# When the last expert's tokens are finished: a mixture-of-experts layer with all outputs written before the last expert is added, and the chosen rows written again by a scatter

## The chip, the cores and the metric

The kernel runs on one core of a Trainium2 chip. The core has five engines that run side by side, each with its own queue of instructions: TensorE (PE: matrix products), VectorE (DVE), ScalarE (ACT), GpSimd (POOL) and SyncE (SP, which here only issues transfers). The metric is the device time of one execution in microseconds (us); lower is better. Line numbers such as L1570 are lines of the kernel before.

## What is computed

4 sequences of 1024 tokens of 256 numbers, float32 (4096 tokens in all), pass two attention layers and two feed-forward layers. Each of the four is applied as `x = x + layernorm(layer(layernorm(x)))`. Only the last is touched by the change. It is a mixture of eight experts in which the experts choose tokens:

```
xt = layernorm(x).reshape(4096, 256)
S  = sigmoid(xt @ Wg).T                # 8 experts x 4096 tokens
G, I = top_k(S, 1024)                  # each expert takes 1024 tokens
hid = gelu(xt[I] @ W1[e] + b1[e])      # 256 -> 1024
out = (hid @ W2[e] + b2[e]) * G        # 1024 -> 256
new = zeros.at[I].add(out)             # a token may have several experts, or none
x = x + layernorm(new)
```

## The kernel before

The tokens stand in SBUF for the whole run, as eight blocks `xs[0]` to `xs[7]` of 512 tokens (128 partitions x 4 x 256). Normalised rows and the gate scores go to a table in device memory, `tok_d`; a second table, `acc_d`, of 4096 rows of 256, starts at zero and collects the experts' sums.

The experts run one after the other, each in two halves of 512 tokens (`feed_forward(u)`, u from 0 to 15; expert e = u // 2). For an expert, GpSimd gathers its 1024 rows from `tok_d` in eight chunks of 128 (`got`, L1493). A half then does this: TensorE turns four chunks to `xT` (L1516, copied by VectorE, L1518), computes `ph` for eight slices of the hidden layer (L1534, 16 matmuls in two per slice, three PSUM buffers), ScalarE applies Gelu (L1541), and TensorE computes `py` for each of the four chunks (L1556, two PSUM buffers). VectorE adds the bias (L1568) and multiplies by the gate (L1569), and GpSimd adds the chunk's rows to `acc_d` with an accumulating scatter (L1570). The turning of the next half's chunks stands on TensorE between the second and third, and the third and fourth, `py`.

The orders on PE, DVE and ACT are written out by hand: within this part an engine runs its instructions in the order in which the code issues them. GpSimd's and SP's queues are laid out by a scheduler. Scatter-adds of different chunks into `acc_d` wait for one another, except those of the last expert, whose tokens are distinct.

After the experts stands a separate last part (L1598 to L1647). Every read of `acc_d` waits for all scatters of the last expert (`last_scatters`); then, block by block:

- SP reads the block's sums back to SBUF (`back`, L1610)
- VectorE computes mean and variance of each token (`bn_stats`, `bn_aggr`, in `ln_stats`, L179 to L182), GpSimd raises the variance to the power -1/2 (L184) and multiplies it by the negative mean (L1631)
- ScalarE applies the scale and shift (L1619), and the result is added to `xs[t]` and stored: for the first four blocks by an accumulating transfer into the output (L1645), to which the rows of `xs[t]` were stored during the attention layer (L1166, `ADDED = 4`); for the others by an add on GpSimd or VectorE (L1624) and a store (L1625).

Of the kernel before, what the change touches and what calls it, by code (L numbers as in the profile page):

```python
# [9 lines left out]
F32 = mybir.dt.float32  # L10
I32 = mybir.dt.int32
BF16 = mybir.dt.bfloat16
AF = mybir.ActivationFunctionType
# [5 lines left out]
P = 128  # L19
D = 256  # L20
# [25 lines left out]
CAP = 2  # L46
NSEG = P // NE
NROUND = 15
ADDED = 4


def bucket_runs():
# [19 lines left out]
def kernel(  # L72
# [956 lines left out]


    tok_d = dram.tile([NT, D + NE], F32, name="tok_d")
    spare = const.tile([P, 1], F32, name="spare")
    with ExitStack() as st3:

# [83 lines left out]
        def close(t, h, oT):  # L1118
# [43 lines left out]
                return scale_of("g", xs[t][:, i, :])  # L1162

            def token_rows(i, mean, rs):
                if t < ADDED:
                    nc.sync.dma_start(out_flat[t][:, i, :], xs[t][:, i, :])  # L1166
                if i == 0:
                    gating["h"] = wk.tile([P, NJ, D], F32, tag="hg", name="hg")
                hg = gating["h"][:, i, :]
                nc.vector.tensor_scalar(hg, xs[t][:, i, :], mean, rs, ALU.subtract, ALU.mult)  # L1170
                nc.sync.dma_start(tok_d[t * TB + i * P : t * TB + (i + 1) * P, 0:D], hg)
                if i % 2:
                    beside.append(lambda: turn_gating(i - 1))
                if i == NJ - 1:
                    beside.append(gate)
# [133 lines left out]
    with ExitStack() as st4:  # L1309
# [132 lines left out]
        class List:  # L1442
# [43 lines left out]
            def gather(self):  # L1486
                nc.tensor.matmul(parts[:, P : P + NC], lhsT=self.listed, rhs=fold, start=True, stop=True)  # L1487
                self.idx = wk.tile([P, NC], I32, tag="idx", name="idx")
                nc.vector.tensor_copy(self.idx, parts[:, P : P + NC])  # L1489
                self.got = []  # L1490
                for c in range(NC):
                    g = wk.tile([P, D + NE], F32, tag="got", name="got", bufs=2 * NC)
                    nc.gpsimd.indirect_dma_start(  # L1493
                        out=g,
                        out_offset=None,
                        in_=tok_d[:, :],
                        in_offset=bass.IndirectOffsetOnAxis(ap=self.idx[:, c : c + 1], axis=0),
                        bounds_check=NT - 1,
                        oob_is_err=True,
                    )  # L1500
                    self.got.append(g)

        lists = [List(e) for e in range(NE)]
        last_scatters = []
        QPE = NC // NJ
        xT = {}

# [12 lines left out]
        def feed_forward(u):  # L1520
# [6 lines left out]
            for h in range(TB // n):  # L1527
# [3 lines left out]
                for f in range(FC):  # L1531
# [12 lines left out]
                    if coming is not None and h == TB // n - 1:  # L1544
                        if f == 1:
                            coming.chunks()
                        elif 2 <= f < 6:
                            coming.places(f - 2)
            if coming is not None:
                for part in range(4):  # L1550
                    coming.collect(part)
            for i in range(NJ):
# [11 lines left out]
                    coming.gather()  # L1564
                if i in (1, 2) and u + 1 < NE * QPE:
                    turn(u + 1, i - 1)
                y = wk.tile([P, D], F32, tag="y", name="y", bufs=4)
                nc.vector.tensor_tensor(y, py, mb2[:, e, :], ALU.add)  # L1568
                nc.vector.tensor_scalar(y, y, lists[e].got[k][:, D + e : D + e + 1], None, ALU.mult)  # L1569
                scatter = nc.gpsimd.indirect_dma_start(  # L1570
                    out=acc_d[:, :],
                    out_offset=bass.IndirectOffsetOnAxis(ap=lists[e].idx[:, k : k + 1], axis=0),
                    in_=y,
                    in_offset=None,
                    bounds_check=NT - 1,
                    oob_is_err=True,
                    compute_op=ALU.add,
                )
                if e == NE - 1:

                    for other in last_scatters:
                        tc.declare_no_dep(scatter.ins, other.ins, reason="an expert's tokens are distinct")
                    last_scatters.append(scatter)

        lists[0].chunks()
        for part in range(4):
# [1 line left out]
            lists[0].collect(part)  # L1588
        lists[0].gather()
        for u in range(NE * QPE):  # L1590
            feed_forward(u)
            e, q = divmod(u, QPE)
            if q == QPE - 1 and e + 2 < NE:
                weights.append(load_expert(e + 2))

    out_rows = out.flatten_outer_dims().rearrange("(t p j) d -> t p j d", p=P, j=NJ)  # L1598
    with ExitStack() as st5:
        wk = st5.enter_context(tc.tile_pool(name="back", bufs=1))  # L1600
        st5.enter_context(tc.manual_schedule(engines={engines.DVE, engines.Activation}))
        all_rows = mybir.DependencyInfo(mybir.DependencyClass.Sync, mybir.DependencyReason.DATA)
        ys = []
        for t in range(NB):
            y = wk.tile([P, NJ, D], F32, name=f"back{t}")
            rows = "(p j) d -> p j d" if t < ADDED else "(j p) d -> p j d"
            acc_t = acc_d[t * TB : (t + 1) * TB, :].rearrange(rows, p=P)

            for js in (slice(0, 1), slice(1, NJ)) if t == 0 else (slice(0, NJ),):
                read = nc.sync.dma_start(y[:, js, :], acc_t[:, js, :])  # L1610
                for scatter in last_scatters:
                    tc.add_manual_dep(read.ins, scatter.ins.name, all_rows, reason="all rows")
            ys.append(y)

        HALVES = (slice(0, NJ // 2), slice(NJ // 2, NJ))

        def apply_on_act(t, tiles, rs, ms):
            for i in tiles:
                nc.scalar.activation(  # L1619
                    ys[t][:, i, :], ys[t][:, i, :], AF.Identity, bias=ms[:, i : i + 1], scale=rs[:, i : i + 1]  # L1620
                )

        def add(t, eng, js):
            eng.tensor_tensor(xs[t][:, js, :], xs[t][:, js, :], ys[t][:, js, :], ALU.add)  # L1624
            nc.sync.dma_start(out_flat[t][:, js, :], xs[t][:, js, :])  # L1625

        for t, y in enumerate(ys):
            mv, rs = ln_stats("c", [y[:, i, :] for i in range(NJ)])
            ms = small.tile([P, NJ], F32, tag="msc", name="msc")
            nc.vector.tensor_scalar(ms, mv[:, :, 0], -1.0, None, ALU.mult)  # L1630
            nc.gpsimd.tensor_tensor(ms, ms, rs, ALU.mult)  # L1631
            if t == NB - 1:

                add(t - 1, nc.vector, slice(0, NJ))
                for i in range(NJ // 2):
                    nc.vector.tensor_scalar(
                        y[:, i, :], y[:, i, :], mv[:, i, 0:1], rs[:, i : i + 1], ALU.subtract, ALU.mult
                    )
                apply_on_act(t, range(NJ // 2, NJ), rs, ms)
                for js in HALVES:  # L1640
                    add(t, nc.vector, js)
                continue
            apply_on_act(t, range(NJ), rs, ms)
            if t < ADDED:
                nc.gpsimd.dma_start(out_rows[t], y, accum_op=ALU.add)  # L1645
            elif t < NB - 2:
                add(t, nc.gpsimd, slice(0, NJ))  # L1647


# [32 lines left out]
```

## The time and the profile before

Three runs had a median of 1663.57 us (1662.66 to 1664.27). The profiled execution took 1663.55 us; its span, from the first to the last instruction that the profile shows, was 1661.6 us at a mean granted TensorE clock of 0.966.

| engine | busy, us | share of the span | instructions |
|---|---|---|---|
| PE (matmul) | 1544.9 | 93% | 8663 |
| DVE | 913.8 | 55% | 2050 |
| ACT | 634.0 | 38% | 1099 |
| POOL | 390.5 | 23% | 419 |

| the end of the span | us from its start |
|---|---|
| expert 7, first half: first `ph` | 1566.4 |
| expert 6's last scatter issued | 1571.1 |
| expert 7, second half: first `ph` | 1594.8 |
| last `py` ends | 1622.6 |
| last scatter issued | 1623.7 |
| first statistics of the last part | 1630.1 |
| last add ends | 1658.3 |
| span ends | 1661.6 |

How to read rows of the timeline: start in us, duration in us, engine, line, operation, what it writes and reads, how many; in brackets how long the engine was idle before, and what ended that. A page's group rows give busy time and the mean duration in ns.

### The profile page before, as it was taken

The page shows a single profiled execution, that of the slowest core. Times are in us where ns is not written, and L with a number is a line of the kernel's source. Part 1 is how long each engine was busy: PE and PEld are TensorE (multiplying, and loading weights), DVE is VectorE, ACT ScalarE, POOL GpSimd, SP SyncE. Part 2 cuts the span into 40 slices and gives each one's busy share as a digit, 9 for nine tenths or more (in the row PEclk, how much of TensorE's full clock was granted, in tenths as well). Part 3 has the DMA queues.
Part 4 walks back from the last instruction along what each step waited for, and adds up shares of the span by engine and source line. Part 5 has one row for each costly group of instructions (what it writes and reads, how often), then busy time and mean ns, then how long its engine had stood idle before and what let it go on. Part 6 is the DMA issues. An engine that isn't in the chain of part 4 may idle for free.

```text
span 1661.6 us, 22279 instructions
## 1 busy us (share of the span) xinstructions
PE 1544.9 (93%) x8663; PEld 769.6 (46%) x8663; DVE 913.8 (55%) x2050; ACT 634.0 (38%) x1099; POOL 390.5 (23%) x419
## 2 busy tenths in 40 slices
PE   7999999999999999999999999914999999999990
PEld 4666666675223232323232222203766766667670
DVE  4555556664567777778787878775121222212115
ACT  3344444544554545454545464421112121121213
POOL 4222233222102011111010101012332432433325
PEclk9999999999999999999999999956999999999995
DMA  8300000000000000000000000030233323423217
GB/s 210 109 1 1 1 1 1 1 1 0 1 1 1 17 11 17 11 14 14 14 14 1 14 8 7 28 128 26 65 68 73 69 66 74 95 47 79 32 19 209
DMA packets 66196, 64.31 MB, mean 39 GB/s; under 512 B 23181, under 2 KB 60074, under 8 KB 65962
## 3 DMA queue, kind: packets, MB, share of 16 engines
q1 hardware_dynamic: 52352, 42.81, 8.4%
q0 software_dynamic: 12864, 19.14, 6.9%
q8 instruction: 68, 1.11, 0.3%
q10 hardware_dynamic: 874, 0.93, 0.2%
q14 instruction: 38, 0.31, 0.1%
HBM read 39.64 MB, written 23.23 MB: 38 GB/s over the span
## 4 chain that ended last, share of the span: by engine, by line
PE 90%; issue 3%; DVE 3%; POOL 2%; DMA 1%; ACT 1%; SPq 0%; POOLq 0%; ACTq 0%; DVEq 0%
PE sc L1223 16%; PE po L1239 15%; PE py L1556 13%; PE ph L1534 13%; PE py L792 3%; PE pg L684 3%; PE pv L700 3%; PE pt L1127 2%; PE ph L848 2%; PE po L764 2%; PE pv L373 2%; PE pq L349 2%; PE pq L869 2%; PE po L768 2%; PE pk L349 1%
## 5 line engine op out<-in xcount | busy, mean ns | idle before, releaser
L1233 DVE TENSOR_SCALAR w<-sc 128x1024 f32<-128x1024 f32 x256 | 312.8, 1222 | 97.3 <-PE sc L1223 65.1
L1232 ACT ACTIVATE w<-sc 128x512 f32<-128x512 f32 x512 | 277.9, 595 | 229.7 <-PE sc L1223 102.6
L1223 PE MATMUL sc<-qT,kT 32*128 32x512 f32 x2048 | 293.6, 640 | 1.5 <-ACT w L1232 0.8
L1239 PE MATMUL po<-w,vaug 128*17 128x512 f32 x2048 | 274.7, 598 | 1.3 <-DVE turned L1271 0.3
L1556 PE MATMUL py<-w,hid 128*128 128x256 f32 x1024 | 230.1, 380 | 0.0
L1541 ACT ACTIVATE hid<-ph,mb 128x512 f32<-128x512 f32 (+1 forms) x136 | 90.0, 662 | 365.7 <-PE ph L1534 365.7
L1534 PE MATMUL ph<-xT,w 128*128 128x512 f32 (+1 forms) x544 | 225.0, 572 | 0.5 <-DVE xT L1518 0.4
L1556 PEld LDWEIGHTS py<-w,hid 128*128 128x128 f32 x1024 | 191.2, 190 | 31.9 <-issue 7.5
L1223 PEld LDWEIGHTS sc<-qT,kT 32*128 32x128 f32 x2048 | 80.8, 183 | 184.9 <-issue 170.7
L1534 PEld LDWEIGHTS ph<-xT,w 128*128 128x128 f32 x544 | 104.8, 193 | 111.6 <-issue 107.6
L1570 POOL DMA_INDIRECT acc_d<-y,idx x64 | 100.8, 1575 | 212.3 <-issue 151.2
L1568 DVE TENSOR_TENSOR y<-py,mb 128x256 f32<-128x256 f32 x64 | 26.8, 419 | 184.4 <-PE py L1556 184.4
L1239 PEld LDWEIGHTS po<-w,vaug 128*17 128x17 f32 x2048 | 35.3, 95 | 200.3 <-issue 171.0
L1493 POOL DMA_INDIRECT got<-tok_d,idx x64 | 65.8, 1028 | 152.7 <-DVE idx L1489 135.6
L1518 DVE COPY xT<-tp 128x512 f32<-128x512 f32 (+1 forms) x34 | 22.4, 660 | 96.8 <-PE tp L1516 96.8
L1059 POOL TENSOR_TENSOR rsg<-veg,mhalf 128x1 f32<-128x1 f32 x32 | 17.7, 553 | 219.5 <-DVE veg L1058 219.5
L792 PE MATMUL py<-wo,oT 128*128 128x256 f32 x256 | 61.9, 385 | 0.0
L684 PE MATMUL pg<-nT,wh 128*128 128x512 f32 x128 | 60.5, 604 | 1.5 <-ACT nT L623 1.5
L700 PE MATMUL pv<-wh,nT 128*128 128x512 f32 x128 | 59.7, 593 | 0.0
L1489 DVE CAST idx<-parts 128x8 int32<-128x8 f32 x8 | 1.3, 167 | 101.8 <-PE parts L1487 101.8
L792 PEld LDWEIGHTS py<-wo,oT 128*128 128x128 f32 x256 | 47.4, 190 | 17.2 <-issue 9.4
L565 POOL TENSOR_TENSOR x<-x,y 128x1024 f32<-128x1024 f32 x14 | 32.9, 2352 | 73.3 <-ACT y L554 73.3
(262 smaller groups left out, 1854.0 us busy)
## 6 DMA issues: line engine op xcount, KB each, us to landing
w<-in_L_ffn_W_dram SPq DMA_DIRECT2D x16, 1024.0 KB, 5.7
x<-in_L_attn_x_dram SPq DMA_DIRECT2D x8, 512.0 KB, 5.0
acc_d<-logits SPq DMA_DIRECT2D x8, 512.0 KB, 5.0
tok_d<-hg SPq DMA_DIRECT2D x32, 128.0 KB, 1.8
back<-acc_d SPq DMA_DIRECT2D x7, 512.0 KB, 8.9
out_dram<-x SPq DMA_DIRECT2D x16, 128.0 KB, 1.7
out_dram<-back POOLq DMA_DIRECT2D x4, 512.0 KB, 6.5
out_dram<-x SPq DMA_DIRECT2D x3, 512.0 KB, 3.2
```

What stands on the lines that cost most here:

```text
L684: nc.tensor.matmul(pg, lhsT=wh[:, c, HID + e * P : HID + (e + 1) * P], rhs=d["nT"][:, c, :], start=(c == 0), stop=(c == DC - 1),)
L700: nc.tensor.matmul(pv, lhsT=d["nT"][:, c, i * P : (i + 1) * P], rhs=wh[:, c, 0:HID], start=(c == 0), stop=(c == DC - 1),)
L792: nc.tensor.matmul(py, lhsT=d["oT"][:, e, :], rhs=wo[:, e, :], start=(e == 0), stop=(e == EC - 1))
L1223: nc.tensor.matmul(sc, lhsT=row["kT"][t][rows, r, kt * P : (kt + 1) * P], rhs=row["qT"][rows, t, qh * TB : (qh + 1) * TB], start=True, sto ...
L1232: nc.scalar.activation(w[:, j, :], sc, AF.Relu)
L1233: nc.vector.tensor_scalar(w[:, 2:4, :], pair, 0.0, None, ALU.max)
L1239: nc.tensor.matmul(po[32 * j : 32 * j + HD + 1, :], lhsT=row["v"][:, kt, HQ * t + 2 * j + r, :], rhs=w[:, j, :], start=(kt == 0), stop=(kt ...
L1493: nc.gpsimd.indirect_dma_start(out=g, out_offset=None, in_=tok_d[:, :], in_offset=bass.IndirectOffsetOnAxis(ap=self.idx[:, c : c + 1], axi ...
L1534: nc.tensor.matmul(ph, lhsT=w1[:, c, f * P : (f + 1) * P], rhs=xT[u][:, c, h * n : (h + 1) * n], start=(c == 0), stop=(c == DC - 1),)
L1541: nc.scalar.activation(hid[:, f, h * n : (h + 1) * n], ph, AF.Gelu, bias=mb1[:, e * FC + f : e * FC + f + 1])
L1556: nc.tensor.matmul(py, lhsT=hid[:, f, i * P : (i + 1) * P], rhs=w2[:, f, :], start=(f == 0), stop=(f == FC - 1),)
L1570: scatter = nc.gpsimd.indirect_dma_start(out=acc_d[:, :], out_offset=bass.IndirectOffsetOnAxis(ap=lists[e].idx[:, k : k + 1], axis=0), in_ ...
```

## The change

The sums in `acc_d` without the last expert are complete once expert 6's last scatter has landed. The change finishes all tokens from these sums while the last expert runs, and finishes the 1024 tokens that the last expert chose a second time, in SBUF, with its contribution:

- While attention runs, the blocks `xs[t]` are stored to a new table `x_d`; the early stores to the output are gone, and so is `ADDED`.
- In expert 6, after its first half, GpSimd gathers the rows of `x_d` that expert 7 chose (`xg`, eight chunks).
- At the start of expert 7 SP reads six blocks of `acc_d` into free buffers (two more later), and GpSimd gathers the chosen rows of `acc_d` (`accg`, eight chunks).
- Between the steps of expert 7, at places set by a table (`asides`), the eight blocks get statistics, power, scale, add and store; the chosen chunks get the bias times the gate (`chosen_known`).
- In expert 7 `py` times the gate is added to `accg` in one VectorE operation, in place of bias, gate and scatter-add. The chunks of its first half are finished during the second half, those of the second half one by one (`chosen_out`): statistics, power, subtraction, multiplication and addition to `xg`, and a plain scatter of the rows over the output. The first of these scatters waits for all block stores.
- The separate last part is gone.

TensorE's instructions and their order are the same as before. The order of the steps in the last expert, by the code: block statistics 0 and 1 follow Gelu 6 and 7 of the first half; statistics 2 to 5 follow its four `py`, and 6 and 7 follow Gelu 0 and 1 of the second half. ScalarE's two halves of a block's scaling come one and two places later, the second of them with the block's add and store.

```diff
             def token_rows(i, mean, rs):
-                if t < ADDED:
-                    nc.sync.dma_start(out_flat[t][:, i, :], xs[t][:, i, :])
...
+                if i == NJ - 1:
+                    nc.sync.dma_start(x_d[t * TB : (t + 1) * TB, :].rearrange("(j p) d -> p j d", p=P), xs[t])
...
+        def stats_of(tag, tiles):
...
+            for i, s in enumerate(tiles):
+                nc.vector.bn_stats(st[:, i, :], s)
+            for i in range(n):
+                nc.vector.bn_aggr(mv[:, i, :], st[:, i, :])
+            nc.vector.tensor_scalar(ve[:, :n], mv[:, :n, 1], EPS, None, ALU.add)
+            nc.gpsimd.tensor_tensor(rs[:, :n], ve[:, :n], mhalf[:, :n], ALU.pow)
+            return mv, rs
+
+        def read_back(t):
+            y = room_back[t % len(room_back)]
+            nc.sync.dma_start(y, acc_d[t * TB : (t + 1) * TB, :].rearrange("(j p) d -> p j d", p=P))
+            ys[t] = [y]
+
+        def all_stats(t):
+            y = ys[t][0]
+            mv, rs = stats_of("c", [y[:, i, :] for i in range(NJ)])
+            ms = few.tile([P, NJ], F32, tag="msc", name="msc")
+            nc.vector.tensor_scalar(ms, mv[:, :, 0], -1.0, None, ALU.mult)
+            nc.gpsimd.tensor_tensor(ms, ms, rs, ALU.mult)
+            ys[t] += [rs, ms]
+
+        def all_scaled(t, half):
+            y, rs, ms = ys[t]
+            for i in (2 * half, 2 * half + 1):
+                nc.scalar.activation(
+                    y[:, i, :], y[:, i, :], AF.Identity, bias=ms[:, i : i + 1], scale=rs[:, i : i + 1]
+                )
+
+        def all_out(t):
+            nc.vector.tensor_tensor(xs[t], xs[t], ys[t][0], ALU.add)
+            stores.append(nc.sync.dma_start(out_flat[t], xs[t]))
+            if t + len(room_back) < NB:
+                read_back(t + len(room_back))
+
+        def chosen_known(ks):
+            for k in ks:
+                nc.vector.scalar_tensor_tensor(
+                    accg[:, k, :], mb2[:, NE - 1, :],
...
+        def chosen_out(ks):
+            mv, rs = stats_of("d", [accg[:, k, :] for k in ks])
+            for i, k in enumerate(ks):
+                nc.vector.tensor_scalar(accg[:, k, :], accg[:, k, :], mv[:, i, 0:1], None, ALU.subtract)
+            for i, k in enumerate(ks):
+                nc.vector.scalar_tensor_tensor(
+                    xg[:, k, :], accg[:, k, :], rs[:, i : i + 1], xg[:, k, :], ALU.mult, ALU.add
+                )
+                scatter = nc.gpsimd.indirect_dma_start(
+                    out=out_rows,
+                    out_offset=lists[NE - 1].at_chunk(k),
+                    in_=xg[:, k, :],
...
+                for store in stores:
+                    tc.add_manual_dep(scatter.ins, store.ins.name, over, reason="in the place of")
...
+        def with_last_rows():
+            for c in range(NC):
+                lists[NE - 1].fetch(xg[:, c, :], x_d, c)
+
+        def with_last_acc():
+            for tag in ("w1", "w2"):
+                free = we.tile([P, 2, NJ, D], F32, tag=tag, name=f"back_{tag}")
+                room_back.extend(free[:, k] for k in range(2))
+            room_back.extend(wk.tile([P, NJ, D], F32, tag="back", name="back") for _ in range(2))
+            for t in range(len(room_back)):
+                read_back(t)
+            for c in range(NC):
+                lists[NE - 1].fetch(accg[:, c, :], acc_d, c)
+
+        def asides():
...
+            places = [(0, "f", 6), (0, "f", 7), *((0, "i", i) for i in range(NJ)), (1, "f", 0), (1, "f", 1)]
+            later = [(0, "f", 7), *((0, "i", i) for i in range(NJ)), (1, "f", 0), (1, "f", 1), (1, "f", 2)]
+            latest = [*((0, "i", i) for i in range(NJ)), (1, "f", 0), (1, "f", 1), (1, "f", 2), (1, "f", 3)]
+            for t in range(NB):
+                put(later[t], lambda t=t: all_scaled(t, 0))
+                put(latest[t], lambda t=t: all_scaled(t, 1), lambda t=t: all_out(t))
+                put(places[t], lambda t=t: all_stats(t))
+            put((0, "f", 7), lambda: chosen_known((0, 1)))
+            put((0, "i", 0), lambda: chosen_known((2, 3)))
+            put((1, "f", 4), lambda: chosen_known((4, 5)))
+            put((1, "f", 5), lambda: chosen_known((6, 7)), lambda: chosen_out((0, 1, 2, 3)))
...
-                y = wk.tile([P, D], F32, tag="y", name="y", bufs=4)
-                nc.vector.tensor_tensor(y, py, mb2[:, e, :], ALU.add)
-                nc.vector.tensor_scalar(y, y, lists[e].got[k][:, D + e : D + e + 1], None, ALU.mult)
...
+                gates = lists[e].got[k][:, D + e : D + e + 1]
+                if e < NE - 1:
...
+                else:
+                    nc.vector.scalar_tensor_tensor(accg[:, k, :], py, gates, accg[:, k, :], ALU.mult, ALU.add)
+                    aside(u, "i", i)
+                    if q:
+                        chosen_out((k,))
...
         for u in range(NE * QPE):
+            if u == (NE - 1) * QPE:
+                with_last_acc()
             feed_forward(u)
             e, q = divmod(u, QPE)
+            if u == (NE - 1) * QPE - 2:
+                with_last_rows()
...
-    with ExitStack() as st5:
```

The last line stands for the whole last part, L1598 to L1647, which is removed.

## The prediction, made before the changed kernel ran

> **What bounds the kernel now.** I read the page first: TensorE is busy 93% of the span, and the chain that ended last is 90% PE. The change cannot shorten TensorE's work, so I looked for where TensorE is not the chain. In the timeline's last 100 us that is the stretch after its last matmul:
>
> ```profile
> 1608.58 13.98 PE L1556 MATMUL py<-w,hid 128*128 128x256 f32 x64
> 1623.68 1.55 POOL L1570 DMA_INDIRECT acc_d<-y,idx  x1 [1.90 <-DVE y L1569]
> 1627.86 6.79 SPq L1610 DMA_DIRECT2D back<-acc_d  x9
> 1631.62 0.43 DVE L179 BATCH_NORM_STATS2 stc<-back 128x6 f32<-128x256 f32 x1 [0.87 <-DMA back<-acc_d]
> 1656.97 1.32 DVE L1624 TENSOR_TENSOR x<-x,back 128x512 f32<-128x512 f32 x2
> ```
>
> TensorE ends at 1622.56; the span ends at 1661.6. These 39.0 us are the prize: the last scatter must land (1627.5), all of acc_d is read back, and eight blocks are normalised and added. The waits on SP's queue say what holds it, in total, times and longest us: the last expert's scatters.
>
> ```profile
> SPq L1610 <- DMA acc_d<-y,idx: 119.6, 3, 112.6
> ```
>
> What the change must fit into is the last expert: its first half begins at 1566.42, its second at 1594.84, and nothing of it waits today. The second thing to see is GpSimd's queue before that, in expert 6:
>
> ```profile
> 1557.50 1.55 POOL L1570 DMA_INDIRECT acc_d<-y,idx  x1 [2.97 <-issue]
> 1562.11 1.55 POOL L1570 DMA_INDIRECT acc_d<-y,idx  x1 [3.05 <-issue]
> 1566.72 1.55 POOL L1570 DMA_INDIRECT acc_d<-y,idx  x1 [3.06 <-issue]
> 1571.14 1.55 POOL L1570 DMA_INDIRECT acc_d<-y,idx  x1 [2.87 <-issue]
> ```
>
> Each scatter-add waits for the one before to land, one per 4.5 us. The queue is behind (the y for the last was ready at 1567.4), so any work put between them moves the last one.
>
> **Removed.** Of the 39.0 us tail, what must remain after the last matmul is one chunk: accg (0.46), its statistics (0.85: 0.43, 0.18, 0.17 and gaps), the power (0.55, the mean of L1059's 128x1), xg (0.46), 0.3 to issue, the landing (2.8 for a gather, 3.8 for a scatter-add; I take 3.5) and 1.0 to the end of the program (the last store's landing to 1661.6): 7.1 us. Were all else hidden, the span would be about 1630, a gain of 32. The rest of this part is why I do not expect that.
>
> **Added before the last expert.** (1) x_d: eight 512 KB stores replace sixteen of 128 KB on SP's queue, during attention, where DMA moves 1 GB/s in most slices; the last runs beside the weight loads near 1090, but its rows are first needed long after the gathers at 1143.6. Cost 0; if exposed, one landing of 5. (2) Eight gathers of xg. In the built order they stand in GpSimd's queue four after expert 6's first scatter-add and four after its second. One gather takes 1.01 plus 0.30, so four take 5.2, more than the 2.9 that the queue waits anyway; a scatter-add behind gathers is also followed later (5.94 from 1538.00 to 1543.94, against 4.5). Second at 1545.2, third at 1552.3, then 5.9 and four times 4.5: the last at 1576.2 instead of 1571.14. Plus 5.1.
>
> **Added in the last expert.** Now I walk the four queues in built order.
> - GpSimd: eight gathers of accg wait for that scatter-add (1576.2 + 4.5 = 1580.7), and take 8 x 1.31: until 1591.2. The power of block 0 stands behind them. That is the first trouble: power (1.05 alone, mean 1.27 in L184; I take 1.4), product 0.3, so ms of block 0 is there at 1592.9.
> - DVE: block 0 is read by about 1584 (3.7 from issue before), statistics of a block 2.2 (2.4 in the old interleaved order), two of them and two known chunks (0.42 each, STT rows of L1147 less overlap), then accg of py 0 at 1589.4 to 1589.9. TensorE's third py needs that PSUM buffer and started at 1587.39 before: 2.6 late.
> - ACT scales block 0 (4 x 0.52) until 1595.0, and only then DVE can add it: the add (1.23, L1624 of 128x1024) stands in DVE's queue ahead of statistics 2, two known chunks, the xT copy (0.69) and accg of py 1. So the copy ends at 1600.1 and accg of py 1 at 1600.5; TensorE's fourth py waits for it until 1600.6, and behind one more add (1.23) and statistics (2.2) the second xT copy ends at 1604.7. TensorE starts the second half at 1604.3 instead of 1594.84: 9.5 late.
> - Second half: 18 scaling operations are ahead of the first Gelu on ACT, and two stand ahead of and two behind each of the next three, each waiting on DVE's statistics and the power. ph has three PSUM buffers. DVE is now the pace: add + statistics = 3.4, 3.5 to 4 a block with waits. Adds end: block 0 1596.3, block 3 1610.3, block 7 1626.3. Gelu 3 is done at 1624.0, so the last ph ends at 1627.5 instead of 1608.6: 19 us late.
> - Then on DVE: four known chunks 1.7, statistics of four chunks 2.1, four subtractions 1.3, first xg 1631.9; scatters from 1632.1. The store of block 7 has landed by then (1626.3 + 3.2 to 4.5). The plain scatter has no row: I bound it by the gather (1.01 + 0.30) and the scatter-add (1.55 + 0.30), and take the gather's, which does not accumulate either. The four end at 1637.4; the power of chunk 4 is queued behind them; then each chunk goes round power 0.55, xg 0.5, issue 0.28, scatter 1.31 = 2.65. TensorE's last py, done near 1642.5, is not late for that. Scatters of chunks 4 to 7 issue at 1638.8, 1641.4, 1644.1 and 1646.7; plus 3.5 and 1.0.
>
> Sum: span 1651.2, against 1661.6: 10.4 less. From 39.0 - 7.1 = 32 hoped for, 19 go to the late second half and 2 to 3 to chunks queued on GpSimd. Profiled time before is 1663.55, 1.95 over its span, and the median 1663.57: so 1651.2 + 1.95 = 1653.2.
>
> **Two rules weighed against rows.** The shared port. Two pairs of rows from two places:
>
> ```profile
> 1654.06 1.23 DVE L1624 TENSOR_TENSOR x<-x,back 128x1024 f32<-128x1024 f32 x1 [3.30 <-ACT back L1619]
> 1654.17 1.99 POOL L184 TENSOR_TENSOR rsc<-vec,mhalf 128x4 f32<-128x4 f32 x1
> ...
> 1080.26 0.67 POOL L1059 TENSOR_TENSOR rsb<-veb,mhalf 128x1 f32<-128x1 f32 x1 [0.19 <-DVE veb L1058]
> 1080.36 0.48 DVE L1147 SCALAR_TENSOR_TENSOR y<-y,mvb,gam 128x256 f32<-128x256 f32 x1
> ```
>
> The power behind an add waited for it (1.99); the add behind a power did not wait (0.48, its usual time), and the power grew by 0.12. The Trainium skill, SBUF — State Buffer, "SBUF: two separate sides", says that a vector operation with two SBUF inputs and a GpSimd operation that reads SBUF exclude each other for a whole instruction, whoever starts first. By the rule every block's add would also stand behind power and product: 1.25 a block over seven intervals, +9, span 1660; by the row 0 to 0.4. I take the row (hence the 1.4).
>
> The clock. Windows of 2 us around one short pause of TensorE (us, busy of PE, PEld, DVE, ACT, POOL, granted clock, DMA):
>
> ```profile
> 1070.00:1072.00 2.00, 0.55 (x2) 0.53 (x3) 1.36 (x2) 0.00 (x0) 0.00 (x0) 0.95 0.00 0
> 1072.00:1074.00 2.00, 2.00 (x6) 1.55 (x6) 0.00 (x0) 0.00 (x0) 0.00 (x0) 0.50 0.00 0
> 1074.00:1076.00 2.00, 2.00 (x8) 1.65 (x7) 1.34 (x3) 0.00 (x0) 0.00 (x0) 0.70 0.01 3
> 1076.00:1078.00 2.00, 1.88 (x13) 0.92 (x13) 1.47 (x5) 0.58 (x1) 0.03 (x1) 1.00 0.37 129
> ```
>
> A pause of 2.3 us halved the clock and some 3.5 us of work restored it. TensorE: Matmul & The Clock Gate, "Part 1", says an idle window of about 3.4 us throttles; the row says that less can. Here the pauses are 7 us (before the fourth py) and 2.5 us (between ph's). The ph's at 3.4 still fit ACT's pace of 4; the last two and the first py run half: about +2, mostly hidden behind the four scatters. By the rule 0, by the row 0 to 2.
>
> **Rivals.**
> 1. Slower: the clock stays halved to the end. If pauses recur so that four py take 27.6 rather than 13.8, the last py ends at 1627.5 + 3.4 + 27.6 = 1658.5 and the chunk's 7.1 follow: 1665.6, 1667.6 us. It turns to a loss when the second half's py run at half clock for more than 10 of their 14 us. Against it: those four are gapless once the Gelus are there, and the rows recover within 4.
> 2. The port excludes, as the page has it: span 1660, 1662 us, nothing gained; with powers of 1.99 for each, 1666.7.
> 3. Better: expert 6's queue absorbs the gathers (-5), and statistics pack to 2.0: 1644 span, 1646 us.
> 4. The end hides as hoped, because ACT and DVE never make TensorE wait: 1632 us. Against it: DVE's added work alone (eight statistics, eight adds, eight chunks) is some 46 us and cannot begin before 1584.
>
> **Chances.** My schedule within 4 us 0.52; better 0.24; hoped-for end 0.03; port 0.13; slower clock or several costs at their upper ends 0.08. Measurement tells about 0.2% (3.3 us) from no change. Faster by more than that (below 1660.2) 0.86, same 0.08, slower 0.06. The range holds all but the hoped-for end, the slower clock and the last of the port case: 1642 to 1661.5.
>
> **To look for after.** TensorE: a wait before the fourth py of the last expert's first half, released by DVE accg, and ph's about 4 us apart in the second, released by ACT hid. GpSimd: eight accg gathers from about 1581, the first power after them; last scatter-add near 1576. Scatters at the end 2.6 apart. Wrong: if TensorE runs through (then the time is near 1632), if adds are 5.5 apart (port), if py rows are 0.8 us each at a clock of 0.5 to the end.

## The result and the profile after

The changed kernel takes 1651.2 us (median of four runs, 1650.42 to 1651.57); the kernel before took 1663.4 beside it. The ratio is 0.9925, with a 95% interval of 0.9913 to 0.9938: 12 us faster. The forecast was 1653.2, in a range from 1642 to 1661.5. The span of the profiled execution is 1648.8 us, 12.8 less than before, at a granted clock of 0.974.

The last 100 us of the timeline, as before the change (start, duration, engine, line, operation):

```profile
1565.45 13.90 PE L1669 MATMUL ph<-xT,w 128*128 128x512 f32 x32
...
1588.44 3.72 PE L1692 MATMUL py<-w,hid 128*128 128x256 f32 x16 [1.76 <-DVE accg L1718]
...
1597.79 6.29 PE L1692 MATMUL py<-w,hid 128*128 128x256 f32 x16 [5.19 <-DVE accg L1718]
1603.92 7.27 PE L1669 MATMUL ph<-xT,w 128*128 128x512 f32 x16
1611.74 1.98 PE L1669 MATMUL ph<-xT,w 128*128 128x512 f32 x4 [0.56 <-ACT hid L1676]
1617.35 8.46 PE L1669 MATMUL ph<-xT,w 128*128 128x512 f32 x12 [3.63 <-ACT hid L1676]
1625.65 13.98 PE L1692 MATMUL py<-w,hid 128*128 128x256 f32 x64
...
1642.55 1.05 POOL L1579 DMA_INDIRECT out_dram<-xg,idx  x1 [0.81 <-DVE xg L1576]
```

Two sums are to be read here. After TensorE's last matmul (1639.63) only 9.2 us are left, where there were 39.0: 29.8 gained. But that last matmul was at 1622.56 and is now 17.1 later: 29.8 - 17.1 = 12.7, which is, but for rounding, the difference of the spans. TensorE, which had never waited in the last expert, now waits 1.76 + 5.19 + 0.56 + 3.63 = 11.1 us, and behind the long waits it is slow: 6.29 us for a product that takes 3.72.

GpSimd's queue answers to the four scatter-adds shown of before:

```profile
1551.55 1.63 POOL L1708 DMA_INDIRECT acc_d<-y,idx  x1 [0.30 <-issue]
...
1574.44 1.56 POOL L1708 DMA_INDIRECT acc_d<-y,idx  x1 [2.94 <-issue]
1579.03 1.08 POOL L1499 DMA_INDIRECT accg<-acc_d,idx  x1 [3.03 <-DMA acc_d<-y,idx]
...
1588.36 1.01 POOL L1499 DMA_INDIRECT accg<-acc_d,idx  x1 [0.30 <-issue]
1589.39 1.06 POOL L1530 TENSOR_TENSOR rsc<-vec,mhalf 128x4 f32<-128x4 f32 x1
```

The last scatter-add is 3.3 us later than before (1571.14), although this run reached expert 7 one microsecond sooner (1565.45 against 1566.42). The power of block 0 starts as the last gather of accg ends. SP's wait for the scatter-adds (in total, times, longest) is now one, not three. Behind it the block stores (L1555) wait for VectorE, which makes their rows:

```profile
SPq L1535 <- DMA acc_d<-y,idx: 71.4, 1, 71.4
SPq L1555 <- DVE stc L1526: 31.0, 6, 12.2
```

The chain of waits, in order of time (start, duration, what), says what then set the end:

```profile
1588.36 1.01 POOL accg L1499
1589.39 1.06 POOL rsc L1530
...
1592.87 1.23 DVE x L1554
1594.10 1.31 DVE stc L1526 x4
...
1605.17 2.02 POOL rsc L1530
...
1609.15 0.99 ACT back L1549 x2
1610.17 1.23 DVE x L1554
...
1616.73 0.58 ACT hid L1676
1617.35 8.46 PE ph L1669 x12
1625.82 13.83 PE py L1692 x64
```

From the gathers it goes through VectorE, GpSimd and ScalarE round after round, one round for each block, and only then through TensorE, for the last ph's and the last products. VectorE's and GpSimd's steps for the last chunk follow (left out here). The experiments take this chain apart.

### The profile page after: what moved, and what is told of

The parts are those of the page before. It is cut to its first block, busy times and chain, and to the rows that moved or that the text cites. A ratio compares the mean times of both kernels' runs of the same rounds, so it can differ in the third digit from the quotient of the medians.

```text
span 1648.8 us, 22341 instructions
## 1 busy us (share of the span) xinstructions
PE 1550.9 (94%) x8663; PEld 770.9 (47%) x8663; DVE 926.6 (56%) x2090; ACT 634.3 (38%) x1101; POOL 399.7 (24%) x434
## 5 line engine op out<-in xcount | busy, mean ns | idle before, releaser
L1669 PE MATMUL ph<-xT,w 128*128 128x512 f32 (+1 forms) x544 | 228.5, 578 | 4.7 <-ACT hid L1676 4.2
L1708 POOL DMA_INDIRECT acc_d<-y,idx x56 | 88.5, 1580 | 166.5 <-issue 139.5
L1706 DVE TENSOR_TENSOR y<-py,mb 128x256 f32<-128x256 f32 x56 | 23.4, 418 | 142.8 <-PE py L1692 135.5
L791 PE MATMUL py<-wo,oT 128*128 128x256 f32 x256 | 61.9, 385 | 0.0
```

Source lines behind the costliest of these rows:

```text
L791: nc.tensor.matmul(py, lhsT=d["oT"][:, e, :], rhs=wo[:, e, :], start=(e == 0), stop=(e == EC - 1))
L1669: nc.tensor.matmul(ph, lhsT=w1[:, c, f * P : (f + 1) * P], rhs=xT[u][:, c, h * n : (h + 1) * n], start=(c == 0), stop=(c == DC - 1),)
L1708: nc.gpsimd.indirect_dma_start(out=acc_d[:, :], out_offset=lists[e].at_chunk(k), in_=y, in_offset=None, bounds_check=NT - 1, oob_is_err=Tr ...
```

## The experiments

All are the changed kernel with the edit shown, timed in three rounds beside the kernel before, whose median lay between 1663.75 and 1664.14. Ratios are to it. `behind(a, b)` only puts a after b in GpSimd's queue. Starts of expert 7 differ by up to 1.7 us between the profiled runs, before any edit reaches TensorE; so the last column counts from there. The intervals reach some 2 to 3 us to each side: differences of 1 to 2 us between two rows rest on that column and on the ranges of the four runs of each.

| kernel | time, us | ratio, 95% interval | last scatter, us after expert 7's first `ph` |
|---|---|---|---|
| changed kernel | 1651.2 | 0.9925 [0.9913, 0.9938] | 77.1 |
| block finishing left out | 1633.3 | 0.9817 [0.9801, 0.9834] | 59.1 |
| xg gathers spread | 1644.9 | 0.9888 [0.9872, 0.9905] | 70.2 |
| powers first | 1646.4 | 0.9895 [0.9879, 0.9912] | 72.2 |
| products first | 1654.2 | 0.9939 [0.9922, 0.9955] | 79.9 |
| statistics first | 1647.7 | 0.9903 [0.9887, 0.992] | 73.4 |
| TensorE kept busy | 1650.3 | 0.9921 [0.9905, 0.9938] | 75.7 |
| three orders together | 1639.1 | 0.9851 [0.9835, 0.9868] | 65.3 |
| and Gelus ahead | 1636.4 | 0.9834 [0.9818, 0.9851] | 62.4 |
| and chosen chunks early | 1636.7 | 0.9838 [0.9822, 0.9855] | 62.5 |
| Gelus ahead, end pipelined | 1635.0 | 0.9827 [0.9811, 0.9844] | 61.0 |

**1. What the block finishing costs.** The eight blocks' read back, statistics, scaling, add and store are left out; the chosen rows are finished as in the changed kernel.

```
-            for t in range(NB):
-                put(later[t], lambda t=t: all_scaled(t, 0))
-                put(latest[t], lambda t=t: all_scaled(t, 1), lambda t=t: all_out(t))
-                put(places[t], lambda t=t: all_stats(t))
...
-            for t in range(len(room_back)):
-                read_back(t)
```

> The finishing of the eight blocks is left out of the last expert: no reads of the sums by blocks, no statistics, scaling, add or store (rows that the last expert did not choose are not written); gathers, chosen chunks and scatters stay. Theory (the block steps on VectorE and ScalarE, standing ahead of what TensorE waits for, make the second half 18 us late): TensorE runs almost through, its last py ends near 1624, and the 9.2 us that follow it in the changed kernel's profile give 1635 us. Rival (the gathers on GpSimd and the chunks queued behind scatters are what costs): 1645 us or more.

The timeline of TensorE and the last scatter:

```profile
1595.15 13.90 PE L1663 MATMUL ph<-xT,w 128*128 128x512 f32 x32
1608.88 13.98 PE L1686 MATMUL py<-w,hid 128*128 128x256 f32 x64
1625.77 1.04 POOL L1579 DMA_INDIRECT out_dram<-xg,idx  x1 [0.82 <-DVE xg L1576]
```

No wait is left in TensorE's rows. The finishing that was meant to run beside the last expert costs 17.9 us there, and the scheme without it would gain 30. So the change is a gain of 30 less a bill of 18. The remaining runs ask what the bill is for: work, or order.

**2. GpSimd's queue ahead of the last expert.** The eight gathers of xg, four and four behind two scatter-adds of expert 6, stand one behind each.

```
                         compute_op=ALU.add,
                     )
+                    if e == NE - 2:
+                        if k:
+                            behind(scatter, fetched[-1])
+                        fetched.append(lists[NE - 1].fetch(xg[:, k, :], x_d, k))
+                        behind(fetched[-1], scatter)
...
-            if u == (NE - 1) * QPE - 2:
-                with_last_rows()
```

> The eight gathers of xg stand one behind each scatter-add of expert 6, in the pauses of about 3 us in which GpSimd waits for a landing, instead of four and four behind the first two. Theory (expert 6's last scatter-add, 4.3 late because of them, moves everything behind it): the last scatter-add is back near 1570, all adds come 4 us earlier, 1647 us. Rival (VectorE's and ScalarE's order paces the last expert whatever the start): 1650 to 1652 us.

GpSimd's timeline: a gather now fits into the time for which the queue waits for a landing anyway.

```profile
1565.30 1.59 POOL L1713 DMA_INDIRECT acc_d<-y,idx  x1 [1.70 <-DMA acc_d<-y,idx]
1567.20 1.06 POOL L1499 DMA_INDIRECT xg<-x_d,idx  x1 [0.31 <-issue]
1569.83 1.59 POOL L1713 DMA_INDIRECT acc_d<-y,idx  x1 [1.56 <-DMA acc_d<-y,idx]
1571.73 1.06 POOL L1499 DMA_INDIRECT xg<-x_d,idx  x1 [0.31 <-issue]
1573.82 1.02 POOL L1499 DMA_INDIRECT accg<-acc_d,idx  x1 [1.03 <-DMA acc_d<-y,idx]
```

The last scatter-add is 4.6 us sooner, the first gather of accg 5.2, and the kernel 6.3, 2 more than the theory had. Counted from expert 7's start, the first add comes 5.8 us sooner and the last one 5.5; the rest of the gain is at the end, where the last chunks wait for TensorE no more (0.3 and 0.9 us in the changed kernel). Eight gathers are the same work; their place was worth all they cost.

**3. GpSimd's queue in front of the first power.** Powers and products of blocks 0 and 1 stand ahead of the last four gathers of accg, which are needed much later.

```
-            for c in range(NC):
-                lists[NE - 1].fetch(accg[:, c, :], acc_d, c)
+            fetch_acc(range(4))
...
+            put((0, "f", 7), lambda: fetch_acc(range(4, NC)), lambda: chosen_known((0, 1)))
```

> On GpSimd the powers and products of blocks 0 and 1 stand behind four of the eight gathers of accg instead of behind all eight. Theory (the first add waits for gathers that nothing needs yet): first power near 1584.5 instead of 1589.4, first add near 1588.4 instead of 1592.9, 1647 us. Rival (a later wait takes its place, the scalings ahead of the Gelus): no more than 1 us, 1650 us.

As the theory had it: 4.8 us less. The first power starts at 1586.51, in a run that reached expert 7 1.7 us later than the changed kernel did, and the second half starts at 1599.67 instead of 1603.92.

**4. TensorE's second half started sooner, and nothing else.** VectorE's block steps of the first half's four products stand behind the fourth product instead of between them.

```
+            known = at[0, "i", 0].pop()
+            at[0, "i", NJ - 1] = [step for i in range(NJ) for step in at.pop((0, "i", i))]
+            at[0, "i", 0] = [known]
```

> On VectorE the block steps of the first half (adds and statistics between the py) all stand behind the fourth product of py with the gate, so that the copies of xT and the products come first; ScalarE's order is unchanged. Theory (VectorE's sum of work and the 18 scalings ahead of the first Gelu pace the second half, not its start): TensorE starts the second half near 1595 instead of 1603.9 but then waits for the first Gelu; the time stays within 2 us of 1651. Rival (TensorE's late start sets the end): 8 us less, 1643 us.

The timeline shows what became of the 5.8 us (counted from expert 7's start) by which the second half is earlier:

```profile
1599.72 5.31 PE L1672 MATMUL ph<-xT,w 128*128 128x512 f32 x12
1615.00 5.59 PE L1672 MATMUL ph<-xT,w 128*128 128x512 f32 x8 [9.96 <-ACT hid L1679]
```

TensorE fills its three PSUM buffers and then waits 9.96 us for the first Gelu, which stands on ScalarE behind the scalings of blocks 0 to 3 and two of block 4. The kernel is 3 us slower by the medians (its four runs, 1651.8 to 1655.1, all lie above the changed kernel's), 1 more than the theory allowed, and the rival's gain of 8 is out. TensorE's late start in the changed kernel is therefore a symptom: the chain of the blocks sets the pace. A block step put off is lost in part: from expert 7's start the first add is 5.8 us later, the last one 4.2, the last scatter 2.8.

**5. The loop in that chain.** A block's statistics stand ahead of the scalings and the add of the blocks before it, at each place of the last expert.

```
             for t in range(NB):
+                put(places[t], lambda t=t: all_stats(t))
+            for t in range(NB):
                 put(later[t], lambda t=t: all_scaled(t, 0))
                 put(latest[t], lambda t=t: all_scaled(t, 1), lambda t=t: all_out(t))
-                put(places[t], lambda t=t: all_stats(t))
```

> One ordering is changed: at each place of the last expert the next block's statistics stand ahead of the block before's scalings and add, not behind them. Theory: the end of the changed kernel is set by a loop, not by the amount of work: add of block t-1, statistics of block t+1 (2.0 us), power and product on GpSimd (2.0), scaling (1.1), Gelu (0.6), second pair of scalings (1.1), add of block t, in all 4.0 to 5 us for each block though no engine has more than 3.5 us to do. With the statistics one place ahead a block costs about 3.6 us of VectorE. Statistics 2 then fill VectorE's 4.5 us wait before the first add, the fourth product starts 2 us sooner, TensorE's waits of 0.6 and 3.6 us in the second half go, and the time is 1645 (6 sooner than 1651). Rival: VectorE's total work sets the end (it has no idle time between 1594 and 1609), so the order gains only the wait it fills: 1649.

3.5 us less, between the two. The adds of blocks 0 to 3 are not sooner (the first hangs on the gathers), but TensorE's second half starts 4.1 us sooner after expert 7's start (34.4 instead of 38.5), block 4's add 1.6 and block 7's 3.2. The add of block 4 in VectorE's timeline, of the changed kernel and then of this one:

```profile
1610.17 1.23 DVE L1554 TENSOR_TENSOR x<-x,back 128x1024 f32<-128x1024 f32 x1 [1.92 <-ACT back L1549]
```

```profile
1609.28 1.22 DVE L1554 TENSOR_TENSOR x<-x,back 128x1024 f32<-128x1024 f32 x1
```

The wait of 1.92 for the scaling is gone. Block 7's add still waits 2.77 for one, and TensorE still waits for Gelus, 1.0 to 2.0 us four times in the second half; they stand on ScalarE behind scalings.

**6. The clock.** Matmuls of zeros into a bank that nobody reads fill TensorE's waits.

```
+                if u == NE * QPE - 2 and i in (1, 2):
+                    warm((6, 16)[i - 1])
...
+                    if u == NE * QPE - 1 and f in (3, 4):
+                        warm((2, 12)[f - 3])
```

> 36 matmuls of zeros into a bank that nobody reads stand in TensorE's order where it waits: 6 before the third product, 16 before the fourth, 2 and 12 behind ph 3 and ph 4 of the second half; nothing else is changed. They keep TensorE busy, so that its clock does not fall to half. Theory (the loop of the blocks over VectorE, GpSimd and ScalarE sets the end; the clock costs little): the fourth product takes 3.7 us instead of 6.3 and the last ph 5.3 instead of 8.5, but Gelu 0 waits for scalings and the products for VectorE, so the time falls by 0 to 1.5: 1650. Rival: the half clock on the way to the last products is what the second half loses, so the 2.7 + 3.2 us come back: 1645 to 1647.

Windows of 4 us (length, busy of PE, PEld, DVE, ACT, POOL, granted clock, DMA share, GB/s), of the changed kernel and of this one:

```profile
1594.00:1598.00 4.00, 0.21 (x1) 0.21 (x2) 3.96 (x16) 1.28 (x3) 1.44 (x2) 0.78 0.70 215
1598.00:1602.00 4.00, 4.00 (x10) 3.19 (x11) 3.96 (x14) 1.60 (x4) 1.17 (x2) 0.50 0.68 198
```

```profile
1596.00:1600.00 4.00, 2.69 (x18) 2.36 (x17) 3.96 (x14) 1.62 (x4) 1.44 (x2) 1.00 0.84 256
1600.00:1604.00 4.00, 4.00 (x16) 2.76 (x16) 3.96 (x15) 0.66 (x2) 2.08 (x2) 1.00 0.78 249
```

The fourth product takes 3.72 instead of 6.29 us, and twelve matmuls of the last ph's 5.6 instead of 8.46. That is 5.4 us of matmul time back, less 1.2 for ph 3 and ph 4, which took 2.83 and 2.33 instead of 1.98 (the clock fell to 0.69 in the window from 1612). The median moves by 0.9, within the intervals. From expert 7's start, the last products begin 2.2 us sooner (58.0 instead of 60.2), the first scatter of a finished chunk not at all (61.9 in both), and the last scatter 1.4 sooner. So most of it was slack. VectorE's column shows why: 3.96 of 4 us busy in the window at half clock as in the one at full clock.

**7. The three orders together** (edits 2, 3 and 5).

> Three orderings together: the last expert's x rows gathered one behind each scatter-add of the expert before; powers and products of blocks 0 and 1 ahead of the last four accg gathers; statistics one place ahead. Theory (nothing but these orders keeps the block finishing from fitting beside the last expert): VectorE needs about 36 us from 1577.6, so the chosen rows of the first four chunks are ready near 1615, TensorE's waits go, its last product ends near 1623 as with the block finishing left out, and the time is 1634 to 1637. Rival (the block finishing itself, its bandwidth and its port sharing, costs time whatever the order): no better than the sum of single gains less overlap, 1641 to 1644.

12 us less than the changed kernel; the single gains of 6.3, 4.8 and 3.5 add to 14.6, so they overlap by 2.5, and the rival's 1641 is beaten. It is 2 us short of the theory. TensorE again, second half:

```profile
1601.90 1.98 PE L1680 MATMUL ph<-xT,w 128*128 128x512 f32 x4 [0.63 <-ACT hid L1687]
1604.97 1.98 PE L1680 MATMUL ph<-xT,w 128*128 128x512 f32 x4 [1.08 <-ACT hid L1687]
1608.96 5.40 PE L1680 MATMUL ph<-xT,w 128*128 128x512 f32 x8 [2.01 <-ACT hid L1687]
1614.20 13.98 PE L1703 MATMUL py<-w,hid 128*128 128x256 f32 x64
```

**8. Gelus ahead.** Scalings and adds of blocks 4 to 7 one place later, so that a Gelu does not wait behind a scaling that waits for GpSimd.

```
+            later[4:] = [(1, "f", f) for f in range(4)]
+            latest[4:] = [(1, "f", f) for f in range(1, 5)]
```

> As the three orderings together (1639.1), with one more: scalings and adds of blocks 4 to 7 one place later, so that Gelu f of the second half stands ahead of the scalings that it waited for. Theory (VectorE's and GpSimd's order ahead of the last products sets the end, no longer TensorE): TensorE's waits of 0.6, 1.1 and 2.0 us and its low clock at 1610 to 1614 go, the last products start at 1608 to 1610 instead of 1614.2, but add 7 still ends near 1610, the first four chosen chunks near 1616, and their four scatters hold the power of the fifth chunk until 1621; the last scatter moves from 1631.1 to about 1630: 1638, a gain of 1. Rival (TensorE's waits for Gelu are what is left over the run without block finishing): the 5 us of the last products' start come back whole: 1634 to 1635.

2.8 us less, between the theory's 1 and the rival's 4 to 5. The last products start at 1608.57, as with no block finishing at all, and then wait for VectorE:

```profile
1620.74 3.72 PE L1705 MATMUL py<-w,hid 128*128 128x256 f32 x16 [1.43 <-DVE accg L1736]
```

The end now hangs on VectorE's and GpSimd's work for the chosen chunks, as the theory said, but add 7 ended at 1608.9 and not near 1610.

**9. Chosen chunks early.** The first four chosen chunks' statistics ahead of adds 5 to 7; product and statistics of each of the last four ahead of the store of the one before.

```
-            put((1, "f", 4), lambda: chosen_known((4, 5)))
-            put((1, "f", 5), lambda: chosen_known((6, 7)), lambda: chosen_out((0, 1, 2, 3)))
+            at[1, "f", 2].insert(0, lambda: chosen_known((4, 5, 6, 7)))
+            at[1, "f", 3].insert(0, lambda: waiting.append(chosen_out((0, 1, 2, 3))))
+            put((1, "f", 5), lambda: chosen_stored(*waiting.pop()))
...
-                        chosen_out((k,))
+                        ready = chosen_out((k,))
+                        if waiting:
+                            chosen_stored(*waiting.pop())
+                        waiting.append(ready)
```

> As the run with the Gelus ahead, and the first four chosen chunks' statistics and subtractions ahead of adds 5 to 7, in VectorE's wait for the scalings; the fifth chunk's product and statistics ahead of its store, and so on by one chunk, so that a power on GpSimd is not behind a scatter that waits. Theory: then TensorE alone sets the end: last product near 1622.5, last scatter 1626 to 1627, end 6.3 us later: 1634.5 to 1636, within 3 us of the run without any block finishing (1633.3), which then costs next to nothing. Rival (the eight blocks' reads and stores, 8 MB in 50 us, or the port sharing slow the scatters and products themselves): no better than 1637.

No gain; the theory missed by 1 to 2. The first xg is ready at 1612.2, yet:

```profile
1616.59 1.07 POOL L1588 DMA_INDIRECT out_dram<-xg,idx  x1 [6.92 <-DVE accg L1743]
```

The profile names VectorE's accg, but the scatter waits for more than one semaphore. Block 7's store was issued at 1611.9, some 3 us later than in run 8, since its add now stands behind the statistics, and it landed 3.8 us after that, at 1615.71:

```profile
L1561 SPq DMA_DIRECT2D out_dram<-x x6: 372/375/800, 1595.6 to 1611.9; - x6
DMA to landing us min/median/max: 3.8/3.8/3.8
```

In the trace GpSimd's queue passes its wait for that landing at 1615.7, and the scatter starts 0.9 later: it had to wait for the store.

**10. The end pipelined, with the first four chunks back behind add 7.**

```
-            at[1, "f", 2].insert(0, lambda: chosen_known((4, 5, 6, 7)))
-            at[1, "f", 3].insert(0, lambda: waiting.append(chosen_out((0, 1, 2, 3))))
-            put((1, "f", 5), lambda: chosen_stored(*waiting.pop()))
+            put((1, "f", 5), lambda: chosen_known((4, 5, 6, 7)), lambda: chosen_stored(*chosen_out((0, 1, 2, 3))))
```

> As the run with the Gelus ahead (1636.4); the last four chunks are pipelined by one (product and statistics of chunk k+1 ahead of the store of chunk k), and the first four chosen chunks stay behind add 7, unlike in the run that moved them ahead (1636.7). Theory: that run lost its gain because add 7 came 3 us later in VectorE's order and the first scatter waits for the landing of block 7's store (issued 1612, landed 1615.7, scatter 1616.6); here the first scatter starts at 1614.2 and the last four follow in steps of 1.9 instead of 2.5, so the last one is at 1626.2 instead of 1628.05: 1634.5. Rival (GpSimd's and the queue's own time for scatters and powers is used up in either order, or scatters beside late stores are slower): 1636.4 again.

```profile
1614.19 1.07 POOL L1588 DMA_INDIRECT out_dram<-xg,idx  x1 [0.81 <-DVE xg L1585]
...
1626.57 0.98 POOL L1588 DMA_INDIRECT out_dram<-xg,idx  x1 [0.30 <-issue]
```

First and last scatter are within 0.4 of where they were expected (1614.2, 1626.2), and so is the time, within 0.5; the steps of the last four are 1.9, 2.6 and 1.5, as chunk 7 now waits 0.6 for TensorE. This version beats the kernel before by 29 us and the changed one by 16; it is 1.7 us above the run with no block finishing. Counted from expert 7's start the last scatter is 1.9 later than there: 1.0 of it stands ahead of the last product's end, the rest behind it, where the last scatter stands behind that of chunk 6 in GpSimd's queue.

Of the bill of 18, then, some 16 were order, and less than 2 is left for the work itself: its eight statistics and adds, its reads and stores, and the shared port. That counts run 1 as it stands. Run 1 was not timed with these orders; TensorE never waits there and the last scatters follow its products, so they should have had little to gain.

## Why the prediction was right

**The main sum.** Forecast: 39.0 - 7.1 = 32, less 19 for the late second half, less 2 to 3 for chunks queued on GpSimd, leaves 10.4. Measured in the same terms: 39.0 - 9.2 = 29.8, less 17.1, less nothing for the queue, leaves 12.7. Each term missed by about 2 us, one against the other two, so that the time came within 2.0 is in part luck. The mechanism, gathers that hold the first power and VectorE that holds the rest, is shown by runs 2, 3 and 5; runs 4 and 6 show that TensorE's lateness goes with it and by itself sets little.

**GpSimd's queue.** Plus 5.1 was forecast for the scatter-adds; plus 4.3 came, when the sooner start is counted (the step behind the last gathers of xg was 4.7 and not 5.9). Gathers of accg came every 1.33 us, against 1.31, and the first power 0.8 before the sum had it (1589.39 against 1591.2, of which 1.0 is the start).

**VectorE's pace.** The last add ended near 1622.1, against 1626.3. A statistics group took 1.9 to 2.0, not 2.2, the first power and product 1.3, not 1.7, and the start was 1.0 sooner. From the end of add 3 to that of add 7 the rounds took 15.8 us against 16.0, but not for the reason given: the forecast had four adds and four statistics there, 13.6 us of VectorE's work, and 2.4 of waits; measured are three statistics and 5.1 us of waits for scalings (1.92, 1.91 and 1.31). The wait for that loop, which run 5 loosens, is what the forecast had too small.

**The end.** This is the term of the sum that was mis-sized. "7.1 us" after the last matmul was 9.2, in run 1 too (1622.86 to 1632.1). The plain scatter took 0.97 to 1.07 on GpSimd, like a gather, as chosen. Up to the last scatter the chunk's steps took 2.9 us against 2.6; from xg's end to the scatter there are 0.3 us, as taken (the 0.81 in its row is GpSimd's idle time since the power, while VectorE makes xg). But from the last scatter's start to the end of the span there are 6.25 us and not 4.5. It is not the landing, for which 3.5 was taken. SP's first instruction behind its wait for the scatters stands at 1645.1, 2.5 us after the start of the last one. What ends last is the closing of GpSimd's own queue, an instruction DRAIN of 5.75 us (count, shortest, median and longest ns, first and last start in us):

```profile
L1766 SPq EVENT_SEMAPHORE  x11: 17/28/28, 1645.1 to 1648.8; - x11
L1766 POOLq DRAIN  x3: 51/102/5749, 1642.3 to 1648.6; - x3
```

The long one starts at 1642.30 and ends at 1648.05, 0.8 before the end of the span. In the kernel before it took 3.72 us, and the last stores landed after it. What it waits for in those 5.75 us stays open.

The steps of 2.65 were 2.5 to 3.5: two of the last three chunks waited 0.3 and 0.9 us for TensorE, which the forecast had called not late; the last chunk was held by TensorE and not by GpSimd's queue, for which it had taken 2 to 3. The last scatter came at 1642.55, 4.15 sooner than forecast, with 1.75 more behind it: together the 2.4 by which the span came out shorter.

**The port.** The row was the right choice. Two chunk steps on VectorE, with two operands in SBUF each, took their usual 0.87 with a power beside them:

```profile
1595.87 0.87 DVE L1562 SCALAR_TENSOR_TENSOR accg<-mb,got,accg 128x256 f32<-128x256 f32 x2
1595.97 1.24 POOL L1530 TENSOR_TENSOR rsc<-vec,mhalf 128x4 f32<-128x4 f32 x1 [3.99 <-DVE msc L1542]
```

Had each excluded the other for a whole instruction, as the Trainium skill states (SBUF — State Buffer, "SBUF: two separate sides"), either the second step would have waited a microsecond for the power, or the power (1.01 alone) would have ended 1.0 after both steps, at 1597.7; it ended at 1597.21. The other way round it does hold: a power that begins just after an add takes 1.92 to 2.02 (1605.16 and 1613.41), and the first of these stands on the chain that ended last. Whether an add waits for a power, this kernel did not try: none began more than 0.12 us before the end of one. Run 2 did:

```profile
1599.57 1.01 POOL L1534 TENSOR_TENSOR rsc<-vec,mhalf 128x4 f32<-128x4 f32 x1 [1.96 <-DVE msc L1546]
1599.80 1.21 DVE L1558 TENSOR_TENSOR x<-x,back_w 128x1024 f32<-128x1024 f32 x1
```

The add began with 0.78 us of the power still to run and took its usual time, and so did the power. The rival that gave 1662 is out: the adds are not 5.5 apart but 2.5 to 5.1, and the two of 5.1 waited 1.9 for a scaling.

**The clock.** "About +2, mostly hidden": run 6 puts it at 0.9 to 1.4. Some near hits are misses that cancel. The fourth product started 2.8 us sooner than forecast (1597.79 against 1600.6) and took 2.6 longer at a clock of 0.50, so the second half began at 1603.92 against 1604.3 (the forecast's own sum has the second copy of xT end at 1604.7, 0.4 behind that start). Gelu 3 was done 4.2 sooner (1619.84 against 1624.0), but the last ph's ran slow, so the last products began only 1.9 sooner (1625.65 against 1627.5). The rival of a clock that stays halved did not come: from 1626 the windows are at 1.00.

**The hidden end.** The forecast gave it 0.03, because VectorE's added work "cannot begin before 1584". For this kernel that was near enough (1582.2). The limit was itself the order of the gathers: with them spread, VectorE begins at 1577.3 (run 10), and the time is 3 us above the 1632 of a hidden end.

## What to carry to other kernels

Work that is moved beside a busy engine is paid for at the places where it stands in the other queues, not by its amount: here some 16 of 18 us were order. An end that is taken as "landing and a little" may be the closing of the queue that issued the last transfer: look at its last instructions. Where a chain goes round several engines once for each block, look for the step that stands behind the block before it without needing it, and put it one place ahead. A wait or a slow clock of the main engine need not be a cost: first see which queue it waits for, and whether that queue has idle time.

## What the runs showed of the hardware

How long TensorE may pause before the granted clock falls was not a matter of the pause alone. Behind pauses of 5.19 and 3.63 us it stood at 0.50 in the changed kernel. In run 2, pauses of 1.46, 2.01, 2.02 and 2.02 us between ph's left it at 1.00; in run 7, pauses of 0.63, 1.08 and 2.01 brought it to 0.57:

```profile
1606.00:1610.00 4.00, 1.98 (x4) 0.68 (x4) 3.06 (x13) 2.65 (x6) 1.97 (x2) 1.00 0.40 132
```

```profile
1610.00:1614.00 4.00, 4.00 (x7) 1.64 (x6) 4.00 (x10) 1.73 (x3) 0.00 (x0) 0.57 0.39 131
```

TensorE is half idle in the first, of run 2, and at full clock; it never pauses in the second, of run 7, and is slow. The Trainium skill (TensorE: Matmul & The Clock Gate, "Part 1") has the clock halve after an idle window of about 3.4 us, and such windows run free of the program; here pauses of at most 2.01 us were enough in run 7. Pauses that fall differently in such windows might explain the difference between the two runs, but no run here varied that alone, and it stays open.

In the changed kernel's last expert a plain scatter took GpSimd 0.97 to 1.07 us, a gather 1.01 to 1.08, and an accumulating scatter of expert 6 1.55 to 1.63. From the last scatter's start to the end of the span there are 6.2 to 6.3 us in all eleven kernels that end in a plain scatter, and in each GpSimd's closing DRAIN ends 5.4 to 5.5 us after that start.
